# A LayerNorm's row of deviations: spread by transposes on TensorE, or fetched over DRAM

## The chip, the cores and the metric

The kernel runs on one core of a Trainium2 chip. The metric is the device time of one execution in microseconds (us). A core has five engines that run side by side, each with its own queue of instructions: PE (TensorE, matrix products and transposes), DVE (VectorE), ACT (ScalarE), POOL (GpSimd) and SP (SyncE, which here only issues DMAs). PEld is PE's loading of weights, which can run beside its products. POOL and ACT can issue DMAs too. Engines wait for each other by semaphores.

## The reference, cut to what matters

```python
# x: (32, 56, 56, 128) float32, 32 images of 3136 tokens with 128 channels
x = x + conv_ref(gn(x), gamma, beta, W)      # group norm, batch norm, signs, 3x3 convolution of signs
t = tokens(x)
t = t + attn_ref(ln(t), w_qkv, w_proj, b_proj)   # "first LayerNorm"; windows of 64 tokens, 4 heads, causal
t = t + ffn_ref(ln(t), gate_w, gate_b, weight1, weight2)  # "second LayerNorm"; 64 experts, top 8 tokens each

def ln(v, eps=1e-5):
    m = mean(v, axis=-1); s = var(v, axis=-1)
    return (v - m) / sqrt(s + eps)
```

In the expert part every expert chooses 8 tokens of an image by a softmax over its tokens, pools them by their weights, runs a small two-layer network on the result and adds it back to those tokens.

## The kernel before, in words

**Prologue** (pools prep, xs, xps, wps). The weights are loaded and prepared, the mean is taken out of them beforehand, so that the LayerNorms need only the deviation. Then x is read once, 16 loads of 3136 KB on SP's queue (L294), transposed by PE (L299) and its statistics are taken by DVE (L301), which gives the thresholds of the convolution's signs.

**Main loop.** The images are taken in 16 pairs (NPAIR), each in 7 blocks of 8 rows (NB, RB), so 112 blocks (N). A block has 448 tokens of each of two images; a unit is 64 tokens of both images, 128 together, and a block has 7 units (NU). The loop over `n` is written out by hand and is software pipelined: in one turn it works on several blocks at once. The order of instructions on every engine is the order in which the program issues them. In turn n stand, in this order:

- `load` of block n+6 (SP),
- `scores` of block n (PE: masks L579, products L590; ACT: the exponentials, L605, two tiles pT),
- the first four taps of the convolution of block n+3 (PE, L509, cv),
- `normalise` of block n+1 (PE: rr, L537; DVE: n1T, L541),
- `gate_logits` of block n-1 (PE, lg, L701; ACT copy L705),
- `attend` of block n (PE, av, L639; DVE: reciprocal rs L647, product ao L651),
- `bits` of block n+5 (PE: xT_ps; ACT L480, L488; DVE L496, L497),
- queries, keys and values of block n+1 (PE L550, L566), between them `turn_out` of block n (PE L662),
- steps of earlier pairs' expert choice (largest logits, gathers, shares),
- `project` of block n (PE pj, L673; DVE tT, L679),
- `norm1` of block n+2 (PE: yt; DVE: statistics L433; POOL: power L426),
- the other five taps and `residual` of block n+3 (ACT L522; DVE L524, L526: yT),
- `norm2` of block n (PE: tt; ACT: tok; DVE statistics, POOL power; stores to out on POOL's queue and to toks on SP's, L692).

**First LayerNorm.** The activations are kept with the channels on the partitions (yT). `norm1` turns the seven units by PE (`turn`, L440), so that the tokens lie on the partitions, and `unit_stats` takes their variance on DVE and the power -1/2 on POOL (ln_rstd, 128 x 7). To multiply yT, the deviations are needed along the free axis in every partition: `normalise` makes this by seven transposes of one column that is read 128 times (`to_broadcast`), into a PSUM tile rr, and DVE multiplies rr by yT. All PSUM tiles of this kind (`bank2`) share three buffers in turn.

**Second LayerNorm's row.** `spread` (L725, L731) does the like for the gate's logits over DRAM on SP's queue, once for six blocks and once for the seventh of a pair: devs is written in token order, and each image's row is read into 64 partitions of drow.

**Shares.** In the steps 8, 9, 10, 12 and 13 after a pair's last block, `shares` builds the table of the pair's weights (8 places; each a compare-and-multiply L874 and, but for the first, an addition L879 on DVE); `store_shares` writes it to DRAM (POOL's queue). The DRAM table has to be zero elsewhere: in turns 1 to 8 of the loop SP writes 1 MB of zeros each (L942).

**End.** After the loop the 64 experts' networks run in 8 parts (their weights are loaded from turn N-4 on), and the results are scattered to the rows of out by POOL's indirect DMAs (L1129).

Of the kernel before, what the change touches and what calls it, by code (L numbers as in the profile page):

```python
# [8 lines left out]
F32 = mybir.dt.float32  # L9
# [8 lines left out]
P = 128  # L18
HEADS = 4
# [11 lines left out]
def kernel(  # L31
# [40 lines left out]

    ident = const.tile([P, P], F32, name="ident")
# [9 lines left out]
    head1 = const.tile([P, HEADS, HD], F32, name="head1")  # L83
# [12 lines left out]
    g4 = const.tile([P, P // 4, 4], F32, name="g4")  # L96
# [12 lines left out]
    tri = const.tile([P, 2, P], F32, name="tri")  # L109
# [54 lines left out]
    with tc.tile_pool(name="prep", bufs=1) as prep, tc.tile_pool(  # L164
# [123 lines left out]


        TP = 2 * S // P  # L290
        x2 = x.rearrange("b h w c -> (b h w) c").rearrange("(n p j) c -> n p j c", p=P, j=TP)
        for pr in range(NPAIR):
            xb = xs.tile([P, TP, C], F32, name="xb")
            nc.sync.dma_start(out=xb, in_=x2[pr])  # L294
            st = xs.tile([P, 2, NB, 6], F32, name="st")
            for g in range(NB):
                pt = xps.tile([P, 2, 512], F32, name="pt").rearrange("p a (s c) -> p (a s) c", c=P)
                for j in range(NU):
                    nc.tensor.transpose(pt[:, j, :], xb[:, g * NU + j, :], ident)  # L299
                for i in range(2):  # L300
                    nc.vector.bn_stats(st[:, i, g, :], pt[:, :NU, i * WIN : (i + 1) * WIN])  # L301
            for i in range(2):
                nc.vector.bn_aggr(
                    mv[:, 2 * pr + i, :], st[:, i].rearrange("p g s -> p (g s)")
                )
            if pr == NPAIR - 4:
                group_norm(0, B - 8)
            if pr == NPAIR - 2:
                scaled(0, B - 8)
        group_norm(B - 8, B)  # L310
# [20 lines left out]


# [3 lines left out]

    share = dram.tile([NQ, P, NPAIR, 2, ES], F32, name="share")
    toks = [dram.tile([2, S, P], F32, name=f"toks{i}") for i in range(NPAIR)]
    eout = dram.tile([E, B, P], F32, name="eout")
    obias_d = dram.tile([P, NG, P], F32, name="obias_d")  # L340
    devs = [dram.tile([2, NB * NU, WIN], F32, name=f"devs{i}") for i in range(NPAIR)]
# [25 lines left out]
    def main_loop(fast):  # L367
        with ExitStack() as main:
# [18 lines left out]
            yTp = loop.enter_context(tc.tile_pool(name="yTp", bufs=4))  # L387
# [22 lines left out]
            zero = first.tile([P, 4 * P], F32, name="zero")  # L410
            nc.gpsimd.memset(zero, 0.0)
# [46 lines left out]
            class Block:  # L458
# [16 lines left out]
                def bits(self):  # L475
# [9 lines left out]
                    bn = w1.tile([P, 2, RB, W], F32, name="bn")  # L485
# [9 lines left out]
                    bit = w1.tile([P, RB, W], FP16, name="bit")  # L495
# [35 lines left out]
                def norm1(self):  # L531
                    self.rstd1 = unit_stats(units(turn(self.yT, "yt")), "ln1")

                def normalise(self):
                    rr = bank2("rr")
                    for u in range(NU):
                        nc.tensor.transpose(  # L537
                            units(rr)[:, u, :], self.rstd1[:, u : u + 1].to_broadcast([P, P]), ident
                        )
                    self.n1T = w1.tile([P, NU, P], F32, name="n1T")  # L540
                    nc.vector.tensor_mul(self.n1T, units(rr), self.yT)  # L541
# [165 lines left out]
            class Pair:  # L707
# [9 lines left out]
                def spread(self, r0, r1):  # L717
# [4 lines left out]
                    dT = wp.tile([m, P], F32, name=f"dT{m}")  # L722
# [7 lines left out]
                    for i in range(2):  # L730
                        nc.sync.dma_start(  # L731
                            out=self.drow[i * E : (i + 1) * E, r0 * BT : r1 * BT],
                            in_=devs[self.pr][i : i + 1, r0 * NU : r1 * NU]
                            .rearrange("o m t -> o (m t)").to_broadcast([E, (r1 - r0) * BT]),
                        )
# [131 lines left out]
                def shares(self, ks):  # L867

                    if ks[0] == 0:
                        self.sh = gatep.tile([P, E, K], F32, name="sh")  # L870
# [27 lines left out]
                def step(self, j):  # L898
# [13 lines left out]
                    elif j == 8:  # L912
                        self.pool()
                        if self.pr < NPAIR - 2:
                            self.shares(range(0, 2))
                    elif j == 9:
                        self.shares(range(2, 3))
                    elif j == 10:
                        self.shares(range(3, 4))
                    elif j == 12:  # L920
                        self.shares(range(4, 6))
                    elif j == 13:
                        self.shares(range(6, 8))
                        self.store_shares()
# [8 lines left out]
            for n in range(-6, N + 1):  # L933
                this, nxt, conv, prev = at(n), at(n + 1), at(n + 3), at(n - 1)
# [51 lines left out]
                if at(n + 5):  # L986
                    at(n + 5).bits()
# [26 lines left out]
                if at(n + 2):  # L1014
                    at(n + 2).norm1()
# [219 lines left out]
```

## Time and profile before

| | us |
|---|---|
| runs: median of 3 (lowest to highest) | 2442.38 (2442.09 to 2454.92) |
| the profiled execution, its own time | 2378.07 |
| its span | 2376.3 |
| its mean granted PE clock | 0.964 |
| the loop's first score mask starts at | 198.06 |
| the loop's last block's score mask starts at | 2118.74 |

The profile is of one execution. Busy times, durations and waits are from it; they are added up against its 2378.07 us, of which 1.8 lie outside the span. In its lines L12 is line 12 of the kernel, `out<-in` are the tiles written and read, xN counts instructions (PE counts records: a float32 product is two, a float32 transpose one), and a bracket gives the idle time ahead of a group and what ended it.

### The profile page before, as it was taken

Reading aid. Unit: us, or ns where it says so; the run is one execution under the profiler, and the core shown is the slowest. Engines: PE = TensorE matmul, PEld = TensorE weight load, DVE = VectorE, ACT = ScalarE, POOL = GpSimd, SP = SyncE. Lnnn points to the kernel's source line nnn. Section 1 sums busy time; section 2 is a strip of 40 time slices with the busy share of each in tenths; the row PEclk is TensorE's granted clock in tenths of the full one; section 3 lists DMA queues with packets and bytes.
Section 4 is the critical chain, followed back from the end, with each engine's and each line's share of the span. In section 5 each row is a group of like instructions: output and inputs, shape, how many; then the busy total and the mean of one; then the engine's idle time right before and its main releaser. Section 6 shows DMA issues by size and latency. Waiting matters only on the chain.

```text
span 2376.3 us, 82834 instructions
## 1 busy us (share of the span) xinstructions
PE 2162.9 (91%) x35865; PEld 1522.2 (64%) x35865; DVE 1778.4 (75%) x4974; ACT 1160.7 (49%) x1683; POOL 814.6 (34%) x772
## 2 busy tenths in 40 slices
PE   6769999999999999999999999999999999973662
PEld 5646666677666667666666766667676666651442
DVE  8975567787878788888887878788888878876331
ACT  0014555556565655555555565655555555532220
POOL 1011224233333333333333242424242424232676
PEclk9989999999999999999999999999999999996776
DMA  9942554645353635353545353636363545475992
GB/s 372 392 157 71 154 156 109 124 92 130 85 136 82 140 80 136 83 130 90 127 93 124 87 135 77 141 76 143 79 138 84 130 92 119 99 216 157 355 342 97
DMA packets 238300, 334.31 MB, mean 141 GB/s; under 512 B 50598, under 2 KB 175206, under 8 KB 231654
## 3 DMA queue, kind: packets, MB, share of 16 engines
q1 hardware_dynamic: 208102, 255.48, 38.6%
q0 software_dynamic: 27648, 72.38, 13.0%
q8 instruction: 285, 4.67, 0.8%
q10 hardware_dynamic: 2176, 1.05, 0.1%
q14 instruction: 89, 0.73, 0.1%
HBM read 195.14 MB, written 134.74 MB: 139 GB/s over the span
## 4 chain that ended last, share of the span: by engine, by line
PE 78%; ACT 7%; DVE 6%; DMA 4%; issue 3%; POOL 2%; SPq 0%; POOLq 0%; DVEq 0%
PE cv L509 9%; PE av L639 8%; PE kT_ps L550 8%; PE pj L673 8%; PE v_ps L566 7%; PE sc L590 7%; PE xT_ps L440 4%; PE lg L701 4%; PE yt L440 4%; ACT bn L488 4%; PE rr L537 4%; PE tt L440 3%; ACT xT L480 3%; DVE st L301 3%; PE sc L579 2%
## 5 line engine op out<-in xcount | busy, mean ns | idle before, releaser
L426 POOL TENSOR_TENSOR ln_rstd<-ln_var,nhalf 128x7 f32<-128x7 f32 x112 | 167.6, 1497 | 926.9 <-DVE ln_var L423 602.4
L480 ACT ACTIVATE xT<-xT_ps,conv_nb 128x896 f32<-128x896 f32 x112 | 112.8, 1007 | 408.4 <-PE xT_ps L440 405.6
L426 POOL TENSOR_TENSOR devs<-ln_var,nhalf 128x7 f32<-128x7 f32 x112 | 165.7, 1479 | 265.9 <-DVE ln_var L423 265.9
L605 ACT ACTIVATE pT<-sc 128x896 f32<-128x896 f32 x224 | 193.3, 914 | 120.1 <-PE sc L590 119.1
L639 PEld LDWEIGHTS av<-vblk,pT 64*64 64x64 f32 x12544 | 196.2, 135 | 86.5 <-ACT pT L605 76.4
L509 PE MATMUL cv<-hbits,wconv 128*128 128x448 f16 x1008 | 233.2, 358 | 12.8 <-DVE s L524 6.1
L566 PEld LDWEIGHTS v_ps<-wqkvT,n1T 128*128 128x128 f32 x1568 | 192.7, 192 | 41.6 <-issue 41.2
L639 PE MATMUL av<-vblk,pT 64*64 64x33 f32 x12544 | 210.2, 221 | 6.3 <-issue 5.5
L679 DVE SCALAR_TENSOR_TENSOR tT<-pj,bproj_c,yT 128x448 f32<-128x448 f32 x224 | 142.8, 679 | 83.8 <-PE pj L673 83.8
L550 PE MATMUL kT_ps<-n1T,wqkvT 128*128 128x448 f32 x448 | 197.7, 564 | 4.6
L673 PE MATMUL pj<-aoT,wprojT 64*128 64x448 f32 x896 | 198.7, 562 | 1.1 <-ACT aoT L665 1.1
L522 ACT ACTIVATE s<-cv,conv_mid 128x448 int32<-128x448 f32 x112 | 70.8, 633 | 257.0 <-PE cv L509 257.0
L566 PE MATMUL v_ps<-wqkvT,n1T 128*128 128x128 f32 x1568 | 193.1, 275 | 0.0
L550 PE MATMUL qT_ps<-n1T,wqkvT 128*128 128x448 f32 x448 | 188.5, 543 | 0.0
L692 POOL DMA_DIRECT2D out_dram<-tok x224 | 169.1, 756 | 0.1
L433 DVE BATCH_NORM_STATS2 ln_st<-yt 128x6 f32<-128x128 f32 x784 | 165.4, 284 | 3.0 <-PE yt L440 3.0
L590 PE MATMUL sc<-qT,kT 32*64 32x64 f32 x12544 | 166.6, 233 | 0.0
L590 PEld LDWEIGHTS sc<-qT,kT 32*64 32x64 f32 x12544 | 151.2, 130 | 22.7 <-issue 22.7
L433 DVE BATCH_NORM_STATS2 ln_st<-tok 128x6 f32<-128x128 f32 x784 | 162.0, 279 | 5.0 <-ACT tok L687 4.9
L488 ACT ACTIVATE bn<-xT_ps,thr_b,thr_a 128x448 f32<-128x448 f32 x224 | 149.4, 720 | 2.8 <-DVE thr_b L330 2.7
L526 DVE SCALAR_TENSOR_TENSOR yT<-s,conv_s,xT 128x448 f32<-128x448 f32 x224 | 143.5, 682 | 4.0
L1129 POOL DMA_INDIRECT out_dram<-f_rows,rowidx x128 | 123.8, 967 | 58.1 <-issue 32.9
(187 smaller groups left out, 4081.7 us busy)
## 6 DMA issues: line engine op xcount, KB each, us to landing
xb<-in_x_dram SPq DMA_DIRECT2D x16, 3136.0 KB
xb<-in_x_dram SPq DMA_DIRECT2D x224, 224.0 KB
toks<-tok SPq DMA_DIRECT2D x224, 224.0 KB
out_dram<-tok POOLq DMA_DIRECT2D x224, 224.0 KB, 3.7
u<-in_L_ffn_weight_dram SPq DMA_DIRECT2D x16, 2048.0 KB
drow<-devs SPq DMA_DIRECT2D x30, 672.0 KB
share<-zero SPq DMA_DIRECT2D x8, 1024.0 KB
grows<-rows SPq DMA_DIRECT2D x32, 256.0 KB
```

Source lines behind the costliest of these rows:

```text
L426: nc.gpsimd.tensor_tensor(rstd, var, nhalf[:, :n], ALU.pow)
L433: nc.vector.bn_stats(st[:, u, :], src[:, u, :])
L440: nc.tensor.transpose(units(t)[:, u, :], src[:, u, :], ident)
L480: nc.scalar.activation(self.xT.rearrange("c i (p j) -> c i p j", j=NU), units(xT_ps).rearrange("c j (i p) -> c i p j", p=WIN), AF.Identity ...
L488: nc.scalar.activation(bn[:, i].rearrange("c h (g j) -> c h g j", j=NU), units(xT_ps)[:, :, i * WIN : (i + 1) * WIN].rearrange("c j (h g) ...
L509: nc.tensor.matmul(self.cv[:, :BT], lhsT=wconv[:, t, :], rhs=hb[:, r * RB + kh : r * RB + kh + RB, kw : kw + W], start=(t == 0), stop=(t = ...
L550: nc.tensor.matmul(pp[:, a, :BT], lhsT=wqkvT[:, s, :], rhs=flat[:, a * BT : (a + 1) * BT], start=True, stop=True,)
L566: nc.tensor.matmul(units(vp)[:, u, :], lhsT=self.n1T[:, u, :], rhs=wqkvT[:, 2, :], start=True, stop=True,)
L590: nc.tensor.matmul(tiles[h // 2][part, h % 2, u * WIN : (u + 1) * WIN], lhsT=left[hp, u, part], rhs=right[hp, u, part], start=False, stop= ...
L605: nc.scalar.activation(pT, rows2(sc), AF.Exp, scale=HD ** -0.5)
L639: nc.tensor.matmul(av[h % 2 * WIN : (h % 2 + 1) * WIN, i, m * VW : (m + 1) * VW], lhsT=self.pT[h // 2][rows, h % 2, u, :], rhs=self.vb[row ...
L673: nc.tensor.matmul(pj[:, i, :BT], lhsT=wprojT[rows, g, :], rhs=self.aoT[rows, :, g, :], start=(g == 0), stop=(g == 1),)
```

## The change

The first LayerNorm's deviations go over DRAM:

- `norm1` turns yT with the tokens in the order of yT's free axis, 7 neighbours to a partition (`c (p u) -> c u p`): each of the seven transposes reads every seventh column. The power's result, 128 x 7, is written to a DRAM tile rdev of the block on POOL's queue.
- a new `spread1`, the last thing in the turn, reads rdev back on POOL's queue as one row of 896 numbers into all 128 partitions of an SBUF tile rr.
- `normalise` has no transposes any more; DVE multiplies yT by that rr.
- `load`, `bits`, the convolution and `norm1` run one block further ahead (n+7, n+6, n+4, n+3), the loop begins at -7, and yT has five buffers.
- The zeros are written in the prologue, after the loads of x, as 8 DMAs of 1 MB from an SBUF tile of 128 x 2048.
- `spread`'s rows are read in pieces of two blocks.
- The shares are spread as 3, 1, 3, 1 over the steps 8, 9, 12, 13 (before 2, 1, 1, 2, 2 over 8, 9, 10, 12, 13).
- Some tiles move between pools (head1, g4, tri, bn, bit, dT, sh); the last pair's sh uses a buffer of the logits.

```diff
@@ prologue
+        zero = prep.tile([P, NPAIR * 2 * ES], F32, name="zero")
+        nc.gpsimd.memset(zero, 0.0)
...
+        for q in range(NQ):
+            nc.sync.dma_start(out=share[q].rearrange("p n i s -> p (n i s)"), in_=zero)
         group_norm(B - 8, B)
...
+    rdev = [dram.tile([P, NU], F32, name=f"rdev{i}") for i in range(NPAIR * NB)]
...
-            yTp = loop.enter_context(tc.tile_pool(name="yTp", bufs=4))
+            yTp = loop.enter_context(tc.tile_pool(name="yTp", bufs=5))
...
                 def norm1(self):
-                    self.rstd1 = unit_stats(units(turn(self.yT, "yt")), "ln1")
+
+                    yt = bank2("yt")
+                    flat = self.yT.rearrange("c u p -> c (u p)").rearrange("c (p u) -> c u p", u=NU)
+                    for u in range(NU):
+                        nc.tensor.transpose(units(yt)[:, u, :], flat[:, u, :], ident)
+                    nc.gpsimd.dma_start(out=rdev[self.n], in_=unit_stats(units(yt), "ln1"))
+
+                def spread1(self):
+
+                    self.rr = w2.tile([P, NU, P], F32, name="rr")
+                    nc.gpsimd.dma_start(
+                        out=self.rr.rearrange("c u p -> c (u p)"),
+                        in_=rdev[self.n].rearrange("(o p) u -> o (p u)", o=1).to_broadcast([P, P * NU]),
+                    )
 
                 def normalise(self):
-                    rr = bank2("rr")
-                    for u in range(NU):
-                        nc.tensor.transpose(
-                            units(rr)[:, u, :], self.rstd1[:, u : u + 1].to_broadcast([P, P]), ident
-                        )
                     self.n1T = w1.tile([P, NU, P], F32, name="n1T")
-                    nc.vector.tensor_mul(self.n1T, units(rr), self.yT)
+                    nc.vector.tensor_mul(self.n1T, self.yT, self.rr)
...
-                    for i in range(2):
-                        nc.sync.dma_start(
-                            out=self.drow[i * E : (i + 1) * E, r0 * BT : r1 * BT],
-                            in_=devs[self.pr][i : i + 1, r0 * NU : r1 * NU]
-                            .rearrange("o m t -> o (m t)").to_broadcast([E, (r1 - r0) * BT]),
-                        )
+                    for r in range(r0, r1, 2):
+                        to = min(r + 2, r1)
+                        for i in range(2):
+                            nc.sync.dma_start(
+                                out=self.drow[i * E : (i + 1) * E, r * BT : to * BT],
+                                in_=devs[self.pr][i : i + 1, r * NU : to * NU]
+                                .rearrange("o m t -> o (m t)").to_broadcast([E, (to - r) * BT]),
+                            )
...
                         if self.pr < NPAIR - 2:
-                            self.shares(range(0, 2))
+                            self.shares(range(0, 3))
                     elif j == 9:
-                        self.shares(range(2, 3))
-                    elif j == 10:
                         self.shares(range(3, 4))
                     elif j == 12:
-                        self.shares(range(4, 6))
+                        self.shares(range(4, 7))
                     elif j == 13:
-                        self.shares(range(6, 8))
+                        self.shares(range(7, 8))
                         self.store_shares()
...
-            for n in range(-6, N + 1):
-                this, nxt, conv, prev = at(n), at(n + 1), at(n + 3), at(n - 1)
+            for n in range(-7, N + 1):
+                this, nxt, conv, prev = at(n), at(n + 1), at(n + 4), at(n - 1)
...
-                if at(n + 6):
-                    at(n + 6).load()
-                if 0 < n <= NQ:
-                    nc.sync.dma_start(
-                        out=share[n - 1].rearrange("p n i s -> p (n i s)").rearrange(
-                            "p (a s) -> p a s", s=4 * P
-                        ),
-                        in_=zero.unsqueeze(1).to_broadcast([P, NPAIR * 2 * ES // (4 * P), 4 * P]),
-                    )
+                if at(n + 7):
+                    at(n + 7).load()
...
-                if at(n + 5):
-                    at(n + 5).bits()
+                if at(n + 6):
+                    at(n + 6).bits()
...
-                if at(n + 2):
-                    at(n + 2).norm1()
+                if at(n + 3):
+                    at(n + 3).norm1()
...
                     this.norm2(pairs[this.pr])
+                if at(n + 3):
+                    at(n + 3).spread1()
```

More of the change, by code (lines that the diff above doesn't have):

```diff
@@ L70 @@
     dram = ctx.enter_context(tc.tile_pool(name="dram", bufs=1, space=bass.MemoryType.DRAM))
+    share = dram.tile([NQ, P, NPAIR, 2, ES], F32, name="share")
+    start = ExitStack()
+    once = start.enter_context(tc.tile_pool(name="once", bufs=1, side="right"))
     ident = const.tile([P, P], F32, name="ident")
@@ L80 @@
     nc.vector.memset(nhalf, -0.5)
-    head1 = const.tile([P, HEADS, HD], F32, name="head1")
+    head1 = once.tile([P, HEADS, HD], F32, name="head1")
     nc.vector.memset(head1, 1.0)
@@ L93 @@
     bounded = const.tile([1, 1], I32, name="bounded")
-    g4 = const.tile([P, P // 4, 4], F32, name="g4")
+    g4 = once.tile([P, P // 4, 4], F32, name="g4")
     nc.vector.memset(g4, 0.25)
@@ L105 @@
     )
-    tri = const.tile([P, 2, P], F32, name="tri")
+    tri = once.tile([P, 2, P], F32, name="tri")
     nc.vector.memset(tri, 0.0)
@@ L330 @@
         nc.vector.tensor_scalar(thr_b, thr_b, off, None, ALU.add)
+    start.close()
     slots = [dram.tile([P, K], F32, name=f"slots{i}") for i in range(NPAIR)]
@@ L335 @@
     grows = dram.tile([NQ, P, NPAIR, P], F32, name="grows")
-    share = dram.tile([NQ, P, NPAIR, 2, ES], F32, name="share")
     toks = [dram.tile([2, S, P], F32, name=f"toks{i}") for i in range(NPAIR)]
@@ L409, in main_loop @@
             nc.gpsimd.memset(vblk, 1.0)
-            zero = first.tile([P, 4 * P], F32, name="zero")
-            nc.gpsimd.memset(zero, 0.0)
             def inverse_std(st, n, name, pool, rstd=None):
@@ L484, in bits @@
                     )
-                    bn = w1.tile([P, 2, RB, W], F32, name="bn")
+                    bn = first.tile([P, 2, RB, W], F32, name="bn")
                     for i in range(2):
@@ L494, in bits @@
                         )
-                    bit = w1.tile([P, RB, W], FP16, name="bit")
+                    bit = first.tile([P, RB, W], FP16, name="bit")
                     nc.vector.tensor_scalar(bit, bn[:, 0], 0.0, 1.0 / FINE, ALU.is_ge, ALU.mult)
@@ L721, in spread @@
                     nc.tensor.transpose(dT_ps, self.devs[:, r0 * NU : r1 * NU], ident)
-                    dT = wp.tile([m, P], F32, name=f"dT{m}")
+                    dT = wp.tile([P, P], F32, name="dT")[:m]
                     nc.scalar.copy(dT, dT_ps)
@@ L869, in shares @@
                     if ks[0] == 0:
-                        self.sh = gatep.tile([P, E, K], F32, name="sh")
+                        if self.pr < NPAIR - 1:
+                            self.sh = wp.tile([P, E, K], F32, name="sh")
+                        else:
+                            sh = gatep.tile([P, S], F32, name="logits")
+                            self.sh = sh[:, : E * K].rearrange("p (e k) -> p e k", k=K)
                     src = self.srow
```

## The prediction

> **What bounds the kernel now.** I read the page from the top: busy shares, the 40 slices, then one stretch by windows, the groups by shape, and the timeline of one block.
>
> ```profile
> PE 2162.9 (91%) x35865; PEld 1522.2 (64%) x35865; DVE 1778.4 (75%) x4974; ACT 1160.7 (49%) x1683; POOL 814.6 (34%) x772
> PE   6769999999999999999999999999999999973662
> ```
>
> Slices 5 to 35 are the main loop over 112 blocks, and PE is full in all of them. The windows say how full; the columns are the stretch, its length, busy us of PE, PEld, DVE, ACT and POOL, the granted clock, the DMA share and GB/s:
>
> ```profile
> 400.00:2000.00 1600.00, 1588.51 (x28220) 1108.46 (x28218) 1295.61 (x3732) 914.50 (x1174) 554.54 (x516) 1.00 0.48 109
> ```
>
> PE is busy 99% at full clock, DVE 81%, DMA 48%. So in the loop a block costs what PE issues for it. From one block's first score mask (1201.38) to the next (1218.48) are 17.10 us. The piece that the change touches (start and length in us, engine, line, operation, records):
>
> ```profile
> 1203.27 0.94 PE L509 MATMUL cv<-hbits,wconv 128*128 128x448 f16 x4
> ...
> 1203.67 1.73 ACT L605 ACTIVATE pT<-sc 128x896 f32<-128x896 f32 x2 [1.29 <-PE sc L590]
> ...
> 1204.04 0.93 PE L537 MATMUL rr<-ident,ln_rstd 128*128 128x128 f32 x7
> ...
> 1204.90 0.97 PE L701 MATMUL lg<-tT,gateT 128*64 128x448 f32 x4
> ...
> 1205.80 1.84 PE L639 MATMUL av<-vblk,pT 64*64 64x33 f32 x112
> ```
>
> While PE runs cv, rr and lg, ACT makes the two exponentials that av reads; they end at 1205.40. The rr transposes thus pay for themselves in part by covering ACT: what is taken out there may come back as a wait of av.
>
> [...] L1076 transposes with a stride of 16 bytes, and its weight loads take longer than the 140 ns of the contiguous ones at L440:
>
> ```profile
> L1076 PEld LDWEIGHTS hT_ps<-ident,hs x64: 195/213/221, 2178.5 to 2317.6; 128*128 128x128 f32 x64
> ```
>
> ```profile
> L440 PEld LDWEIGHTS yt<-ident,yT x784: 137/140/230, 181.4 to 2100.5; 128*128 128x128 f32 x196
> ```
>
> (min/median/max ns.) [...] all 224 of L526 (two SBUF inputs) take 678 to 687 ns, and the one at 1202.70 runs under POOL's power from 1202.31. [...] For out_dram's 224 KB[...] the page shows 3.7 to landing, in traffic.
>
> **The change, part by part, for a full block (n = 1 to 107, where attention, convolution and logits all run).**
>
> *rr leaves PE.* From rr's first start to lg's are 1204.90 - 1204.04 = 0.86 us. Av would then start 0.86 earlier. The second exponential ends 0.68 us before av starts (median over the loop, from the starts in the trace; this block 0.40), so av is now 0.18 ahead of it. Its first four products need only the first exponential (8 records at 1.77/112 = 0.016 us: 0.13). That it goes like this the last block shows, which has neither cv nor rr there:
>
> ```profile
> 2120.89 1.73 ACT L605 ACTIVATE pT<-sc 128x896 f32<-128x896 f32 x2 [1.14 <-PE sc L590]
> ...
> 2121.86 0.32 PE L639 MATMUL av<-vblk,pT 64*64 64x33 f32 x8
> 2122.66 2.07 PE L639 MATMUL av<-vblk,pT 64*64 64x33 f32 x104 [0.49 <-ACT pT L605]
> ```
>
> Eight records, then a wait that ends 0.04 after the exponential. So the wait is 0.18 - 0.13 + 0.04 = 0.09, and -0.77 stays. Bounds: with this block's 0.40 in place of 0.68 the wait is 0.37 and -0.49 stays; without a wait -0.86.
>
> *Strided yt transposes.* By the starts of single records at full clock, L1076 goes at 0.122 us a transpose and 0.223 for the first of a group, contiguous yt at 0.109 and 0.165. Seven: 0.955 - 0.819 = +0.14. The stride becomes 28 bytes; [...] I take the same. Bounds: 0, and +0.67 if each load of 213 ns stood bare (7 x 0.213).
>
> Net -0.63 a block, x 107 = **-67 us**.
>
> *DVE.* n1T now reads two SBUF tiles. L541 takes 1082 ns for 896 elements, L751 with two SBUF inputs 3418 for 3136, which is 1.09 ns an element: no change. Before, DVE waited 0.76 us for av ahead of the reciprocal (L647); 0.63 of this goes, so DVE is the next bound, 0.13 us behind. If POOL's power (1.48) blocked n1T for its whole length, 1.48 - 0.13 - 0.66 (the time from ao's end to aoT's start) = 0.69 would come back; I take 0. The shares: one share is 0.54 + 0.69 = 1.23 us of DVE; step 13, which falls with step 6 of the next pair (2.2 of statistics), goes from two to one, steps 8 and 12 get one more. That lowers the heaviest places: 0.
>
> *POOL.* Two issues more a block, rdev and rr, each about the 756 ns of L692: 1.5 on 4.5 us of 17.1. In the block with gathers (8 x 1.26 us) the powers come about 2 us late. Before, PE's rr stood behind that power; now only rdev does, and nothing in the same block. The rr issue waits for rdev's landing; between them lie devs' power and two stores (4.4 us), about a landing. Behind it stands only the next block's power, before which POOL idles some 10 us. 0.
>
> *The row's way over DRAM.* rr is issued about 1209.0 (end of the out_dram issues), n1T reads it at 1222.9 less the saving: 13 us. [...] drow, also one DRAM row read into many partitions, lands 1.38 MB in about 7 us, 0.81 us for each 10.5 KB packet. At that rate rr's 8 packets an engine take 2.2. Hidden. Share: 112 x 128 x 0.27 us / 16 = 240 us, +10% on 48%[...].
>
> *One block more of lead.* The fill gets one more iteration of bits, convolution and statistics; such iterations took 6.7 and 8.7 us (cv starts 172.01, 178.68, 187.34): +7.7. The end loses that work from loaded iterations: 9 products and 14 transposes, at most 3.5 us of PE, I take 3. **+5**, between 0 and +9.
>
> *Zeroing.* 8 x 1 MB leave the loop, where they were hidden, and stand on SP's queue ahead of the loop's first loads. At 376 GB/s, the prologue's rate, that is 22 us. The windows show DMA at 0.00 from 150 to 160 and the first x transposes at 164.51, while DVE finishes statistics until 161.7. It ends about 160: 0, at worst +6. The memset (four times the 558 ns of L411) comes before ident at 1.1 us; ident is first needed at 7.49: 0. *Row pieces:* four more SP issues of 0.6 us a pair; SP idles: 0, a microsecond or two near the end.
>
> **Sum:** 2378.07 - 67 + 5 = 2316 for the profiled execution. The median of the runs is 64 us above it, at 2442.38; nothing in the page tells why, and I carry the difference unchanged: **2380 us**.
>
> **The rivals.**
>
> *A second bound takes over (DVE or the exponentials).* For it: only 0.13 us of slack on DVE and 0.18 of overrun on ACT. Against: the last block's order above, and L526's even durations. With av's wait at 0.37, or 0.3 us of DVE delay, -0.35 remains: 2442 - 37 + 5 = 2410. With both[...] nothing to speak of: 2435.
>
> *Weight loads set the pace (slower).* Place: yt, on full PE. If a 28-byte stride costs more than 16, each transpose is as long as its load. It decides from (0.77 + 0.82)/7 = 0.227 us a transpose on, twice today's 0.109; at 0.32 (the load of L1076 and half again) a block loses 2.24 - 0.82 - 0.77 = 0.65 and the time is 2442 + 70 + 5 = 2517. For it: a bare load already takes 0.213. Against: in L1076 all but the first overlap, at 0.122.
>
> *The row comes late (slower).* From 14 us between issue and use on, n1T makes qT wait, and each microsecond costs one in every block: at 17, 107 x 2.2 less the gain, +170. Against: 3.7 us for a landing, and POOL mostly idle.
>
> **How the numbers follow.** Main course 0.78 (2360 to 2400); second bound 0.12, of which 0.05 within half a per cent; slower by the loads or the row 0.08; the rest, 0.02, no change. Half a per cent, 12 us, is about what a measurement of this kernel can tell from no change. Faster 0.85, same 0.07, slower 0.08. The range takes the main course, its bounds (no wait, contiguous cost: -92) and the milder second bound: 2352 to 2424.
>
> **What would show it.** The rr group gone; yt at 0.12 to 0.13 us a transpose; av with about eight records and then a wait for pT of about 0.1; blocks 16.5 us apart; the first score about 7 us later; DVE's wait at L647 small; POOL near 43%, DMA about 0.6 in the loop. Blocks at 16.8 or more with DVE or pT named as the releaser mean the second bound; n1T waiting for a DMA means the row; yt at 0.2 the loads. A time over 2424 makes the prediction wrong.

## The result, and the profile after

The change did not pay. In the first comparison the kernel after took 2485.86 us (median of 4 runs) and the kernel before 2446.12 (median of 4): a ratio of 1.016, interval 1.012 to 1.019. The forecast was 2380, range 2352 to 2424. Two later comparisons of the same two kernels are needed to read this: 1.014 (1.012 to 1.016) and 1.000 (0.999 to 1.002). The chips are not alike: in four comparisons the kernel before took 2446 to 2468 us, in two about 2380 (medians). The five later comparisons ran on five chips, one each, and on each of them the runs of before that are compared lie within 20 us. The profiled execution of before, 2378.07, is by its time of the second kind, its timed runs of the first; on which chip they ran is not on record. So the ratios below are to the kernel before on the same chip, and profiles are compared with profiles of the same kind, which I call **with** and **without the hold-up** (its nature comes below).

The page of the kernel after, with the hold-up: busy shares, the slices, and the DMA queue q8, which matters later.

```profile
PE 2156.8 (87%) x35081; PEld 1475.0 (59%) x35081; DVE 1783.2 (72%) x4974; ACT 1161.1 (47%) x1683; POOL 1043.6 (42%) x996
...
PE   6768999899999999999999999999999999944542
...
q8 instruction: 279, 4.57, 0.8%
```

PE issues 784 transposes fewer, and still the loop is longer. The slices don't tell why; they show PE full. The stretch that was shown of before does: PE is busy 95% in place of 99%, at a granted clock of 0.97, and DMA stands at 0.54 in place of 0.48.

```profile
400.00:2000.00 1600.00, 1518.92 (x26444) 1025.47 (x26445) 1245.29 (x3577) 876.71 (x1126) 709.67 (x670) 0.97 0.54 131
```

The block that was shown of before, in an undisturbed place of the kernel after:

```profile
1190.12 1.13 PE L544 MATMUL yt<-ident,yT 128*128 128x128 f32 x7
...
1194.78 0.94 PE L517 MATMUL cv<-hbits,wconv 128*128 128x448 f16 x4
1194.94 1.73 ACT L621 ACTIVATE pT<-sc 128x896 f32<-128x896 f32 x2 [1.02 <-PE sc L606]
...
1195.65 0.97 PE L717 MATMUL lg<-tT,gateT 128*64 128x448 f32 x4
...
1196.55 1.89 PE L655 MATMUL av<-vblk,pT 64*64 64x33 f32 x112
```

rr is gone between cv and lg, the seven yt transposes take 1.13 us (contiguous 0.98), and av takes 1.89 in place of 1.84, so it hardly waits for the exponentials. Such a block is as forecast. The time by blocks shows where the loss is. I took the time from one block's first score mask to the next from the trace, and the medians by the block's place in its pair (0 to 6), over the second to the fifteenth of the 16 pairs:

| profile | place 0 | 1 to 4 | 5 | 6 | half clock in 0 / 5 | fill | loop | end |
|---|---|---|---|---|---|---|---|---|
| before, first (without) | 17.27 | 17.27, 17.13, 17.13, 17.14 | 17.17 | 17.20 | 3 / 0 | 198.1 | 1920.7 | 257.5 |
| before again, e1 (with) | 17.27 | 17.25, 17.12, 17.12, 17.35 | 19.05 | 17.19 | 0 / 7 | 197.9 | 1954.8 | 306.9 |
| after, third, e18 (without) | 19.57 | 16.82, 16.52, 16.55, 16.53 | 17.15 | 16.89 | 17 / 0 | 204.3 | 1924.0 | 254.8 |
| after (with) | 20.33 | 16.87, 16.61, 16.66, 16.67 | 21.32 | 16.89 | 24 / 44 | 205.8 | 1987.9 | 292.6 |

(us; half clock: us at a granted clock of 0.5 in 12 pairs; fill: to the first score mask; loop: to the last; end: from there.) Places 2 to 4 save 0.5 to 0.7 us, as forecast, and places 1 and 6 save 0.3 to 0.45. Place 0 loses 2.3 to 3.1, and place 5 loses 2.3 where there is a hold-up. PE's waits inside the loop name them; the columns are the total, the times and the longest. The kernel after, with the hold-up:

```profile
PE sc L606 <- issue: 31.9, 50, 1.4
PE av L655 <- issue: 29.9, 23, 9.5
PE tt L448 <- DVE tT L695: 11.8, 13, 1.2
```

Without it (e18):

```profile
PE av L655 <- issue: 30.1, 22, 7.8
PE tt L448 <- DVE tT L695: 13.1, 15, 1.2
```

The kernel before, again (e1), with it:

```profile
PE sc L579 <- DVE ln_st L433: 24.9, 14, 2.4
PE av L639 <- issue: 4.3, 4, 2.6
```

So there are three items: PE stops inside av (with or without hold-up), PE waits for DVE's tT (the same), and with the hold-up PE stops inside sc, where the kernel before waits at the score masks. "Issue" means that no semaphore explains the wait. The theory that I went on with: **(A)** the row's transfers do it, by their queue (A1) or their bytes (A2). The rivals: **(B)** the stalls are in both kernels and the first profile missed them; **(D)** the shares make DVE late; **(E)** GpSimd's indirect DMAs hold PE up; **(F)** the burst of the second norm's deviations does it.

### The profile page after: what moved, and what is told of

Its sections match the earlier page's. It is cut to its first block, busy times and chain, and to the rows that moved or that the text cites. A ratio compares the mean times of both kernels' runs of the same rounds, so it can differ in the third digit from the quotient of the medians.

```text
span 2486.3 us, 81658 instructions
## 1 busy us (share of the span) xinstructions
PE 2156.8 (87%) x35081; PEld 1475.0 (59%) x35081; DVE 1783.2 (72%) x4974; ACT 1161.1 (47%) x1683; POOL 1043.6 (42%) x996
## 4 chain that ended last, share of the span: by engine, by line
PE 60%; issue 12%; DVE 11%; POOL 9%; ACT 7%; DMA 1%; POOLq 0%; SPq 0%; DVEq 0%
PE av L655 7%; PE cv L517 7%; PE kT_ps L566 6%; PE sc L606 6%; PE v_ps L582 6%; PE pj L689 6%; POOL out_dram L1144 4%; PE xT_ps L448 4%; ACT bn L496 4%; PE lg L717 4%; PE yt L544 3%; ACT xT L488 3%; DVE st L308 3%; PE qT_ps L566 3%; PE tt L448 2%
## 5 line engine op out<-in xcount | busy, mean ns | idle before, releaser
L434 POOL TENSOR_TENSOR devs<-ln_var,nhalf 128x7 f32<-128x7 f32 x112 | 251.6, 2246 | 171.3 <-DVE ln_var L431 163.8
L655 PEld LDWEIGHTS av<-vblk,pT 64*64 64x64 f32 x12544 | 207.6, 136 | 125.8 <-ACT pT L621 77.3
L655 PE MATMUL av<-vblk,pT 64*64 64x33 f32 x12544 | 225.0, 223 | 37.4 <-issue 33.6
L517 PE MATMUL cv<-hbits,wconv 128*128 128x448 f16 x1008 | 242.0, 368 | 14.7 <-DVE s L532 9.9
L606 PE MATMUL sc<-qT,kT 32*64 32x64 f32 x12544 | 184.3, 239 | 32.9 <-issue 32.9
L606 PEld LDWEIGHTS sc<-qT,kT 32*64 32x64 f32 x12544 | 161.9, 134 | 74.6 <-issue 74.1
L566 PE MATMUL qT_ps<-n1T,wqkvT 128*128 128x448 f32 x448 | 197.7, 565 | 1.5 <-DVE rs L663 0.7
L544 PEld LDWEIGHTS yt<-ident,yT 128*128 128x128 f32 x784 | 105.3, 214 | 71.0 <-ACT vblk L586 53.4
```

Of the source, the lines that this page charges most:

```text
L434: nc.gpsimd.tensor_tensor(rstd, var, nhalf[:, :n], ALU.pow)
L517: nc.tensor.matmul(self.cv[:, :BT], lhsT=wconv[:, t, :], rhs=hb[:, r * RB + kh : r * RB + kh + RB, kw : kw + W], start=(t == 0), stop=(t = ...
L566: nc.tensor.matmul(pp[:, a, :BT], lhsT=wqkvT[:, s, :], rhs=flat[:, a * BT : (a + 1) * BT], start=True, stop=True,)
L606: nc.tensor.matmul(tiles[h // 2][part, h % 2, u * WIN : (u + 1) * WIN], lhsT=left[hp, u, part], rhs=right[hp, u, part], start=False, stop= ...
L655: nc.tensor.matmul(av[h % 2 * WIN : (h % 2 + 1) * WIN, i, m * VW : (m + 1) * VW], lhsT=self.pT[h // 2][rows, h % 2, u, :], rhs=self.vb[row ...
```

## The experiments

Ratios are to the kernel before on the same chip, with 95% intervals.

**e1: the kernel before, unchanged.**

> The kernel before, unchanged. Its profiled execution took 2378 us and its other runs 2442 to 2455; the trace of that execution has few of the stalls of PE that the kernel after shows in two blocks of every pair of images (inside sc's products just after the gathers, and inside av in the block whose deviations are spread). Theory A (the row's way over DRAM makes those stalls): another profiled execution looks like the first, about 2378 us, with under 10 such gaps over 0.6 us inside sc and av between 230 and 2090 us. Theory B (the stalls are there in both kernels, and the first profiled execution of the kernel before happened to miss them): this one is at 2440 to 2455 us and shows them, 40 or more, some 2 us each and followed by stretches of half clock. The time itself is that of the kernel before within 0.5%.

Measured: 1.000 (0.998 to 1.002), 2461.8 us. Neither text fits as a whole. Its stalls are not those of the kernel after (no gap in sc, four in av), but it is 83 us of span longer than the first profile: 34 in the loop, in place 5, and 49 at the end. Place 5, once GpSimd's eight gathers have been issued:

```profile
898.64 1.12 PE L509 MATMUL cv<-hbits,wconv 128*128 128x448 f16 x5
...
899.82 0.96 PE L440 MATMUL tt<-ident,tT 128*128 128x128 f32 x7
900.11 0.94 POOL L802 DMA_INDIRECT rows<-toks,pairidx  x1 [0.30 <-issue]
...
900.70 0.36 PE L579 MATMUL sc<-masks,selw 64*128 64x448 bf16 x2
901.25 1.48 DVE L433 BATCH_NORM_STATS2 ln_st<-yt 128x6 f32<-128x128 f32 x7 [1.58 <-PE tt L440]
902.76 0.63 ACT L522 ACTIVATE s<-cv,conv_mid 128x448 int32<-128x448 f32 x1 [5.58 <-remote]
...
902.78 0.36 PE L579 MATMUL sc<-masks,selw 64*128 64x448 bf16 x2 [1.72 <-DVE ln_st L433]
```

PE's cv ended at 899.76, and ACT, which needs it, starts 3.0 us later: while the last gathers are issued, PE's signals seem to reach the others late. The end, where GpSimd issues 128 indirect stores, is also longer. PE's largest wait there, in the first profile and in this one:

```profile
PE fo L1120 <- DMA logits<-eout: 61.7, 8, 9.8
```

```profile
PE hT_ps L1076 <- DVE hs L1069: 80.2, 7, 16.2
```

This is the hold-up. It goes with the chip, or with the time at which the chip was used (each was used once), and not with the change. It is of the kind and the size of the 64 us between the profiled execution of before and its runs (83 us here); that it is the same thing is likely and not shown.

**e2: the row on SP's queue.**

```diff
-nc.gpsimd.dma_start(out=rdev[self.n], in_=unit_stats(units(yt), "ln1"))
+nc.sync.dma_start(out=rdev[self.n], in_=unit_stats(units(yt), "ln1"))
-nc.gpsimd.dma_start(out=self.rr..., in_=rdev[self.n]...)
+nc.sync.dma_start(out=self.rr..., in_=rdev[self.n]...)
```

> The kernel after, with the two transfers of the row (out to DRAM, back into 128 partitions) issued by SP on its queue in place of GpSimd on its own. The bytes are the same. Theory A1 (the row in GpSimd's software queue, among the gathers and the output's stores, is what starves PE): the stalls in sc and av go, blocks come at 16.6 us in all phases, 112/7 x 9 = some 140 us less at most: 2350 to 2400 us. Theory A2 (the load on the DMA engines does it, whichever queue it comes by): as the kernel after, 2475 to 2500. Theory B (nothing to do with the row): as the kernel after.

Measured: 1.003 (1.002 to 1.005), 2473 us, between the two. PE's "issue" wait in sc falls from 31.9 to 17.1 us, places 0 and 5 to 19.75 and 20.39. The queue has a share; most of the stall in av (29.1 us) stays.

**e3: rr by PE's transposes again, and `norm1` with its order and its turn as in the kernel before; all else as after.**

```diff
 def normalise(self):
+    rr = bank2("rr")
+    for u in range(NU):
+        nc.tensor.transpose(units(rr)[:, u, :], self.rstd1[:, u : u + 1].to_broadcast([P, P]), ident)
-    nc.vector.tensor_mul(self.n1T, self.yT, self.rr)
+    nc.vector.tensor_mul(self.n1T, units(rr), self.yT)
```

> The kernel after without the row's way over DRAM: statistics from contiguous transposes in unit order, deviations spread by seven transposes on PE into PSUM as in the kernel before; the longer lead, smaller row pieces, zeroing ahead of the loop and shares stay as in the kernel after. Theory A: the two stalls per pair go and blocks come at 17.1 us: the time of the kernel before plus the longer fill, 2445 to 2455 (2380 to 2390 if its profile is free of stalls). Theory B (lead, pieces, shares or zeroing do it): the stalls stay and each block costs 0.6 us more than in the kernel after, 2540 to 2560.

Measured: 1.014 (1.011 to 1.018), 2498 us: between again. The stall in av is gone (2.8 us), so it needs the row; but place 0 takes 18.45, for PE's wait for tT (19.1 us, 18 times) is still there, and place 5 alternates between 19.0 and 20.4 to 21.6. The row's way and the rest of the change thus have separate losses. The dearer place 5 has half clock after it (34 us in 12 pairs), the 19.0 has none: whether half clock follows is worth about as much as the hold-up itself.

**e4: two transfers for the deviations' row in place of the pieces.**

```diff
-for r in range(r0, r1, 2):
-    ... [(to - r) * BT] per piece
+... [(r1 - r0) * BT] at once
```

> The kernel after with the deviations of the second norm spread in two transfers of seven (then one) rows' length for each pair, as in the kernel before, in place of eight smaller ones. Theory A (the row does it): as the kernel after within 0.3%, stalls in both phases. Theory C (the six row pieces at once on SP's queue make the stall in the block that issues them): that stall goes, 16 x 4.5 = 70 us less, about 2415, and the one after the gathers stays.

Measured: 1.018 (1.014 to 1.022), 2508 us; place 0 21.2. Theory C falls; no gain or loss by the size of the pieces shows.

**e5: the shares at the steps of before.**

```diff
-8: range(0, 3)  9: range(3, 4)              12: range(4, 7)  13: range(7, 8)
+8: range(0, 2)  9: range(2, 3)  10: range(3, 4)  12: range(4, 6)  13: range(6, 8)
```

> The kernel after with the shares at the steps of the kernel before (2 at step 8, 1 at 9, 1 at 10, 2 at 12, 2 at 13 in place of 3, 1, 0, 3, 1). In the kernel after, and in the run with rr on PE, the first block of each pair (step 8) has PE's tt waiting 0.9 to 1.3 us for DVE's tT in 13 to 18 of 15 pairs; in the kernel before it never waits there. Theory D (the third share at step 8 makes DVE late): this wait goes, 15 x 0.9 to 1.3 = 14 to 20 us less than the kernel after, 1.008 to 1.011 of the kernel before. Theory A (only the row's way costs): no change, 1.016.

Measured: 0.999 (0.998 to 1.001), 2467 us. The wait for tT is gone from PE's list, place 0 falls to 18.50, place 5 stays (21.57). D holds. The gain in the timed runs, 1.5 points or 37 us, is more than the wait says. The medians of place 0 mislead here (20.33 and 18.50; its times fall into two groups): in the mean place 0 takes 1.1 us less (19.98 and 18.90), of which 0.84 is the wait and 0.1 less half clock, and the two loops differ by 16 us. The rest of the 37 us does not show in the profiles and stays open. The place in the trace of e18, step 8 of a pair:

```profile
950.04 0.55 DVE L896 TENSOR_SCALAR sh<-srow,idxf,topv 128x512 f32<-128x512 f32 x1
...
950.62 0.69 DVE L901 TENSOR_TENSOR sh<-sh,sh 128x512 f32<-128x512 f32 x1
951.23 1.27 DVE L695 SCALAR_TENSOR_TENSOR tT<-pj,bproj_c,yT 128x448 f32<-128x448 f32 x2
...
952.65 0.96 PE L448 MATMUL tt<-ident,tT 128*128 128x128 f32 x7 [1.22 <-DVE tT L695]
```

The third share (950.04 to 951.31) stands right ahead of tT, and PE waits 1.22.

**e6: no gathers.**

```diff
-for k in range(K):
-    nc.gpsimd.indirect_dma_start(out=self.rows[:, k, :], in_=toks[pr]..., in_offset=...)
+self.rows = zrows[0]      # set to zero once
```

> The kernel after without the gathers of the chosen tokens' rows (eight indirect DMAs of GpSimd for each pair): their tile is set to zero once and used for every pair, so the chosen rows are left out of the computation. Theory E (PE's instructions and semaphores are held up while GpSimd issues indirect DMAs): the dribble inside sc after the gathers goes, with its stretch of half clock, 15 x 4.7 = 70 us less than the kernel after; the stall in av in the first block of a pair stays, and so does PE's slow pace in the last 200 us, where 128 indirect stores of the output are issued. Theory A2 (bytes on the DMA engines): the gathers are 0.5 MB of the 20 MB a pair moves, so at most 10 us.

Measured: 0.983 (0.980 to 0.986), 2428 us, 3.1 points below the kernel after (1.014): 76 us, forecast 70. This kernel leaves the chosen rows out. Place 5 takes 16.52, place 0 stays at 19.5, the end at 315 us. E holds. In the kernel after the hold-up strikes inside sc:

```profile
1171.93 0.95 POOL L820 DMA_INDIRECT rows<-toks,pairidx  x1 [0.30 <-issue]
...
1172.05 0.45 PE L606 MATMUL sc<-qT,kT 32*64 32x64 f32 x23
...
1172.71 0.29 PE L606 MATMUL sc<-qT,kT 32*64 32x64 f32 x2 [0.21 <-issue]
...
1173.19 1.04 POOL L820 DMA_INDIRECT rows<-toks,pairidx  x1 [0.30 <-issue]
1174.14 0.28 PE L606 MATMUL sc<-qT,kT 32*64 32x64 f32 x2 [1.14 <-issue]
...
1174.87 0.21 PE L606 MATMUL sc<-qT,kT 32*64 32x64 f32 x1 [0.45 <-issue]
...
1175.59 1.62 PE L606 MATMUL sc<-qT,kT 32*64 32x64 f32 x84 [0.50 <-issue]
...
1177.14 1.67 PE L517 MATMUL cv<-hbits,wconv 128*128 128x448 f16 x4
```

Five records in 2.9 us, which no semaphore holds back, and then cv takes 1.67 us in place of 0.94: the granted clock is 0.5 from 1176.25 for 3.41 us. Between 230 and 2090 us the kernel after has 21 such stretches, 17 of 3.41 us, three of 6.83 and one of 10.24, the kernel before two of 3.41; what starts one is not shown.

**e7: the row read into 16 partitions; e8: the deviations read into 16 of 128.**

```diff
e7 -... rdev[self.n]...to_broadcast([P, P * NU])
e7 +... rdev[self.n]...to_broadcast([16, P * NU])     # for n >= 2
e8 -out=self.drow[i * E : (i + 1) * E, ...]
e8 +out=self.drow[i * E : i * E + 8, ...]             # for all pairs but the first
```

> The kernel after with the row of the first norm read back into 16 partitions in place of 128 (but for the first two blocks); the other partitions keep the values of the first two blocks, so the normalisation of later blocks is left wrong in them. The issues on GpSimd's queue and their waits are the same, the bytes an eighth. Theory A2 (the 448 KB a block read from one row of DRAM crowd out PE's instruction pages): the stalls in av of the first block of a pair go, and the dribble after the gathers comes back to the 1.9 us of the kernel before: 15 x (3 + 2.5) = some 80 us less than the kernel after. Theory A1 (the issues in GpSimd's queue, not the bytes): as the kernel after.

> The kernel after with the deviations of the second norm read back into 8 of each 64 partitions for all pairs but the first; the gate's logits of the other partitions are scaled by the first pair's deviations. Theory F (the av stall in the first block of each pair comes from the deviations' broadcast, 1.6 MB from one row of DRAM in a few us, on top of rr's): that stall goes, the first blocks come at 17.8 us (the late DVE stays) in place of 20.3, 15 x 2.5 = 38 us less than the kernel after; the dribble after the gathers stays. Otherwise: as the kernel after.

Measured: 0.998 (0.997 to 1.000) and 0.999 (0.998 to 1.000). In both the stall in av shrinks, from 29.9 us to 17.5 and 11.1, of which one stall in the third pair is 10.8 and 8.1; place 0 takes 18.4 and 18.1, with no half clock. Place 5 stays at 21.3 to 21.4. So A2 is right for av and wrong for sc, and F is right: either traffic alone is borne, both together are not. The DMA view of the kernel after, 956 to 966 us, in 40 slices of a quarter us, and its queues:

```profile
DMA  6999997799999889999999999999997654531078
...
q1 hardware_dynamic: 1529, 2.15, 86.9%
q8 instruction: 1, 0.02, 0.7%
```

The same stretch in PE's timeline:

```profile
961.20 1.84 PE L655 MATMUL av<-vblk,pT 64*64 64x33 f32 x109
...
964.32 0.30 PE L655 MATMUL av<-vblk,pT 64*64 64x33 f32 x3 [1.28 <-issue]
```

All 16 DMA engines are full for 8 us (from 956 to 964 the share is 1.03, each packet counted where it starts). One packet of q8, of 16 KB, falls in it: it started at 962.02 (4.5 us after the block's start) and landed at 963.07; av goes on at 964.3. The kernel after has 279 packets of this queue, all of 16 KB, for 70,871 records of PE, the kernel before 285 for 72,467: 254 records a packet in both. So I take such a packet for a page of PE's instructions. Over 15 pairs, the first page of place 0 starts 2.6 to 5.0 us after the block's start in the kernel after (median 3.7), and 1.4 to 4.0 us in e8 (median 2.3).

No view names the page that PE waits for, but it can be counted. Take PE's records in the order of the trace, weight loads, products and event instructions. Between 230 and 2090 us the kernel after has 15 "issue" waits of over 0.6 us in av and xT_ps. Counted in portions of 256, all 15 begin behind the same record of the portion (192, counted from 0); no other length from 240 to 271 brings them within 90 records of each other. So a portion of 256 is a page here (277 of them). The 15 waits end 1.25 to 1.6 us after a page has landed, whose number among the packets fits the count each time. Of the 16 such waits in sc none begins there. In e18 all 15 of its waits of this kind lie at a page's edge, in each of the two profiles of before all 5 of any line. So PE stands at the edge of a page in av, and the stalls in sc are another thing. The lead is about one page: a page's packet starts 1.6 us (median over the loop; 1.2 in the first profile of before) after PE has entered the page ahead of it, and PE's quickest pages last 3.4 us.

**e9: the kernel after; e10: the row on SP and the shares as before; e11: that, with gathers four and four; e12: the kernel before with gathers four and four.**

```diff
-    ends[5].gather()
+    ends[5].gather(range(0, 4))
+if 6 in ends:
+    ends[6].gather(range(4, 8))
```

> The kernel after, unchanged, timed on the same chip as its variants. All theories: 1.012 to 1.019 of the kernel before, as in its first comparison; first blocks of a pair at 20.3 us, blocks after the gathers at 21.3, the others at 16.6 to 16.9.

> The kernel after with two parts undone together: the row's two transfers on SP's queue, and the shares at the steps of the kernel before. Alone they gave 1.003 and 0.999 of the kernel before. If their gains are separate (queue: the gathers' block; shares: the first block), 0.988 to 0.992; if both only remove the same stretches of half clock, 0.997 to 1.001.

> As the run with the row on SP and the shares as before, and the eight gathers of a pair issued as four in the block where all eight were and four in the next. Without any gather the block after them took 16.5 us in place of 21.3. Theory E1 (PE is held up in proportion to each indirect DMA): two stalls of half the length, under 1.5 us each and without half clock, 15 x 1.5 = some 20 us less than with eight together: 0.980 to 0.985 of the kernel before. Theory E2 (the last gathers of a run hold PE up, whatever their number): two full stalls, 15 x 2 to 4.5 us more: 1.00 to 1.02.

> The kernel before with its gathers split in the same way, four and four. Its block after the gathers takes 19.05 us in place of 17.2. Theory E1: that 1.9 us goes or halves, 15 to 28 us less: 0.988 to 0.994. Theory E2: two stalls of 1.9 us, 1.010.

Measured, on one chip with the hold-up: 1.014 (1.012 to 1.016), 1.002 (1.001 to 1.003), 0.996 (0.995 to 0.997) and 0.994 (0.992 to 0.995). e10 missed its first range and lies just above the second: the two gains don't add up. e11's place 5 falls from 20.4 to 18.4, without half clock, but PE now waits 20.5 us for tT; less came out than expected. e12 came at the edge of E1's range: place 5 takes 17.56, in e1 19.05. That is 0.4 us over the 17.17 without a hold-up, for four gathers, in place of 1.9 for eight: a shorter run holds PE up less than in proportion.

**e13: the deviations in three portions; e14: with gathers four and four; e15: with the shares as before too; e16: with SP's queue too.**

```diff
-if this and this.r == NB - 1 and n < N - 1:
-    pairs[this.pr].spread(0, NB - 1)
+if this and this.r in (2, 4, 6) and n < N - 1:
+    pairs[this.pr].spread(this.r - 2, this.r)
```

> The kernel after with the deviations of the second norm sent out and spread in three portions, in blocks 2, 4 and 6 of the pair (two rows each), in place of one portion of six rows in block 6; the bytes are the same. In the kernel after the DMA engines are full for 9 us around the first block's av, and PE stalls inside av there. Theory F (the burst does it): the stall in av goes, the first blocks come at 17.8 us (the wait for DVE stays) in place of 20.8: 15 x 3 = 45 us less, 0.995 to 0.999 of the kernel before. Theory F2 (the row's own transfer does it, whatever runs beside it): as the kernel after, 1.014.

> As the run before with evened portions, and the gathers split four and four. The block after the gathers, 21.0 us in the kernel after, comes down to 18.4 or below, as in the other run with split gathers: 15 x 2.6 = 39 us less than with evened portions alone, 0.980 to 0.985. If the stall only moves to the second group of gathers: as with evened portions alone.

> As the run with evened portions and split gathers, with the shares at the steps of the kernel before. PE's wait for DVE's tT in the first block goes (0.9 to 1.3 us in 13 pairs): 12 to 16 us less, 0.974 to 0.979. All three causes are then gone and the row is still on GpSimd's queue: the sum of the prediction, -67 + 5 = -62 us, would be 0.975 of the kernel before; if the gathers' block keeps 1.9 us as in the kernel before, the same.

> As the run before, with the row's two transfers on SP's queue. If the queue costs nothing of its own once the bursts are gone: within 0.3% of the run with them on GpSimd's. If GpSimd's issues cost by themselves: 5 to 15 us less.

Measured: 0.995 (0.994 to 0.996), 1.012 (1.010 to 1.014), 1.004 (1.003 to 1.005), 0.997 (0.995 to 0.998). The chip was one without the hold-up (before: 2381 us), so e13's 0.995 is no test of its text, which reckoned with one, and the split, made against the hold-up, could only cost. It cost 40 us (e14 against e13), by DVE's waits, here in e14:

```profile
DVE g_st L844 <- DMA rows<-toks,pairidx: 49.3, 39, 3.6
```

The second four land too late for their statistics, tT comes after these, and place 5 rises from 17.06 to 18.84. What e13 shows all the same: with the same bytes in three portions place 0 takes 18.07 and has no half clock. F2 falls. The portions have a price of their own: places 2 and 4 take 16.88, in e18 16.52 and 16.53. e15 and e16 give back what the share and GpSimd's queue cost here: 0.8 points each.

**e17: three portions, shares as before, row on SP, gathers in one run; e18: the kernel after.**

> The kernel after with evened portions of the deviations, the shares at the steps of the kernel before and the row on SP's queue; the gathers stay eight in one run. On a chip without the hold-up: the run with evened portions alone (0.995) less the first block's wait for DVE (18.07 to 17.0, 16 us) and less what the queue gave (20 us): 0.980 to 0.986. On a chip with the hold-up: the block after the gathers stays at 20.4 in place of 19.05, the others save 0.4 each: 0.988 to 0.994. If the queue gave nothing but shorter waits for the split gathers: 0.988 on a chip without hold-up.

> The kernel after, unchanged. On a chip with the hold-up: 1.012 to 1.019 as twice before. On a chip without it the dribble after the gathers (15 x 4.7 us) is absent and the stall in the first block (some 3.5 us more than with evened portions) stays: the run with evened portions alone took 0.995 there, so 0.995 + 15 x 2.7 / 2381 = 1.010 to 1.014 if only the burst differs, that is, the change does not pay there either.

Measured, again without the hold-up: **0.988 (0.986 to 0.989)**, 2348 us, and 1.000 (0.999 to 1.002). e18 is better than expected by 1 point. e17 misses its first range and meets the last one of its text, by which the queue gave nothing but shorter waits for the split gathers. e17 beats both kernels; on a chip with the hold-up it was not run. Its loop, its av at the place of the stall, and PE's largest wait:

```profile
400.00:2000.00 1600.00, 1563.72 (x28263) 1068.17 (x28265) 1323.53 (x3822) 938.92 (x1227) 642.83 (x526) 1.00 0.53 139
```

```profile
927.23 1.86 PE L655 MATMUL av<-vblk,pT 64*64 64x33 f32 x112
```

```profile
PE dT_ps L737 <- POOL devs L434: 22.6, 58, 1.0
```

The DMA share is about that of the kernel after (0.55 in e18), PE's busy time is back at 98%, and the loop takes 1881.6 us, 39 less than in the first profile of before.

## Why the prediction was wrong

Three terms failed. The shares were put at 0 and cost 13 us. The row's way over DRAM was called hidden, and it cost some 29 us by late pages of PE's instructions and the half clock after them. The 64 us were carried unchanged and grew by 30 to 34 where there is a hold-up.

**rr leaves PE, strided yt transposes: right.** The sum was -0.63 a block. Places 2 to 4 go from 17.13 and 17.14 down to 16.52 to 16.55, -0.60 in the mean; the transposes cost +0.15 (forecast +0.14), av's wait under 0.1. It was counted for 107 blocks; in full it holds in three places of seven, in two more to a half or two thirds.

**DVE: wrong in the shares, and on GpSimd's power.** "That lowers the heaviest places: 0" looked at step 13, and passed over what the third share at step 8 stands in front of. Its own price, 1.23 us, was in the text; it came out as a wait of about 0.9 us (longest 1.2) in 13 to 15 pairs, 12 to 13 us, and e5 gained at least that. I also took 0 for a delay of n1T by GpSimd's power, and looked at one side alone: n1T keeps its 1083 ns, and the power is delayed. In the kernel after, 110 of the 112 powers of devs run beside n1T, whose two inputs are in SBUF, and take 2292 ns (median); the two that do not take 1474 and 1502. In the kernel before, where n1T reads rr from PSUM, 109 run beside it, at a median of 1479. The mean in the kernel after, 2246:

```profile
L434 POOL TENSOR_TENSOR devs<-ln_var,nhalf 128x7 f32<-128x7 f32 x112 | 251.6, 2246 | 171.3 <-DVE ln_var L431 163.8 <-PE av L655 7.4
```

In the kernel after this nearly hides: PE's dT_ps waits for it 3.2 us in all. In e17, with three portions a pair, it waits 22.6 us, in the kernel before not at all; one such wait, 0.39 us, is shorter than the 0.77 us that the power has gained.

**The row's way over DRAM: "hidden" was right of the row and wrong of its bytes.** The row itself is never late (n1T waits 0.3 us, once). But I added 10% to a mean DMA share of 48% and did not ask what the row meets in its own stretch. Around place 0 the deviations' burst keeps the engines busy in the kernel before already (e1: 0.86 from 933 to 946), and what is pushed back there is not a tile but PE's next instructions. Cost without the hold-up, summed over the 16 pairs of e18 and the first profile: place 0 takes 31 us more where 0.63 x 15 = 9 less was forecast, 40 us in all. The parts in e18 are the late share's wait, 13, the waits for pages, some 20, and half clock, some 9.

**POOL: 0 was wrong with the hold-up.** Busy share as forecast (42 to 43%). Yet the row on SP's queue won 1.1 to 1.3 points in e2. Between e15 and e16 it won 0.8, in the places of the split gathers (5: 18.82 to 18.22; 6: 17.70 to 17.21).

**One block more of lead: right.** The first score mask comes 5 to 8 us later (+7.7 forecast ahead of the gain at the end). **Zeroing, row pieces:** 0, and nothing in the runs speaks against it.

**The sum: 64 us carried unchanged: wrong.** They are no constant. With the hold-up, place 5 of the kernel before holds 1.9 us of it a pair and the end 49 us. The change turns the 1.9 into 4.2 (21.32 - 17.15). PE used to wait 1.8 us a pair at the masks; now it stops within sc for 2.3 and loses some 2 by half clock after it: 15 x (4.2 - 1.9) = 34 us. Why it stops there and not at the masks is not shown.

Put together, without the hold-up: fill +6.2, loop +3.3, end -2.7, that is +6.9 between two profiles and a ratio of 1.000. The loop's +3.3, summed over all pairs, is -35.3 in places 1 to 4 and 6, +30.5 in place 0, +2.3 in place 5, and once +5.7 in the third pair. There av stands for 7.8 us (3.1 in the kernel before), again at the edge of a page, while loads in packets of 512 bytes run in turn 14; the DMA share is 0.45 in the 9 us ahead of the stall and 0.69 in the 11 us that hold it (464 to 475), in the kernel after, where av stands for 9.5 us at that place, 0.52 (468.5 to 475.5), so full engines are not the only way to a late page. With the hold-up the two loops differ by 33 us, 30 more than without; measured were 1.4 and 1.6%, 35 and 40 us. e17 saves 30 us of the 62 forecast. What it lacks is PE's wait for devs, 22.6, and 10 us more in the third pair's block (31.9 in place of 22.0).

Of the rivals, DVE as the next bound came true in one place of seven, by the shares; the loads' pace and the row's lateness did not. "The row comes late" had the right resource and the wrong victim.

**Open:** why chips differ in the hold-up, and how GpSimd's indirect DMAs hold PE up; why e5 won more in the timed runs than between the profiles; why place 5 without the hold-up saves nothing (in e18 PE waits there 0.23 us a pair for the exponentials; e17 has 16.73).

## What to carry to other kernels

Where a change adds a transfer, look at the DMA share in the stretch where it will run, not at its mean over the loop, and count the engines' instructions among what the DMA engines carry (here q8, 0.8% of their time): in av, a dense group, PE stopped for up to 9.5 us with no semaphore to blame. Counting its instructions in pages then tells a late page from another stop. Where a profiled execution and the timed runs differ, find out in which stage before adding anything to either; the difference can be in just the stages that the change touches. And when the scarcest engine is relieved, look again at the engine next behind it in every block that is not like the others.

## What the runs showed of the hardware that was not expected

- GpSimd's indirect DMAs hold PE up on some chips: signals of PE seem to come up to 3 us late (e1), or its products go one or two at a time, 0.7 to 1.4 us apart (kernel after); without the gathers (e6) place 5 falls from 21.3 to 16.5 us. On the chips of e13 to e16 and of e17 and e18 it is absent (place 5 of the kernel after: 17.15 against 21.32 us; end: 254 to 260 against 289 to 315).
- PE's instruction pages (q8 by the count in e8's section) are 0.8% of the DMA time, and where the 16 engines are full (1.03 from 956 to 964 us in the kernel after) the first of them starts 3.7 us after the block's start in place of 2.3 (medians, kernel after and e8): every wait of over 0.6 us in av begins at the edge of a page and ends 1.2 to 1.6 us after a page's landing (28 of 28 in the two profiles of the kernel after; all but two last 0.6 to 2.0 us).
- Beside a DVE product of 896 elements with both inputs in SBUF, begun 0.17 us ahead of it, a GpSimd power takes 2292 ns (kernel after), in place of 1479 beside the same product with one input in PSUM (kernel before; medians); the product keeps its own 1083.
- A stall of 2 to 3 us costs more where 3.41 us of half clock follow (1.7 us, half of them, is an estimate); whether they do decided as much as the stall itself (19.0 against 20.4 to 21.6 us in e3).
